# The first block's top layer in two parts of 16 steps, with two products per bank, in a one-core chain of four conditioned layers

## The chip, the cores and the metric

The kernel runs on one core of a Trainium2 chip. The metric is device time in microseconds of one execution. The kernel before took 1318.25 us (median of three runs, 1317.85 to 1321.23).

## What is computed

x is 8 sequences of 512 steps of 256 features; cond is one vector of 256 per sequence. Four residual layers follow each other, all in float32:

```
x = x + L0(x, cond)   # mixture of experts: shared SwiGLU + 2 of 8 routed experts
x = x + L1(x, cond)   # Haar transform, gate(cond), inverse: a gate per feature
x = x + L2(x, cond)   # adapter: low-rank factors generated from cond, gelu between
x = x + L3(x, cond)   # GRU over the 512 steps, output projection
```

L0: `shared = (silu(x sw1') * (x sw3')) sw2`; the router takes `sigmoid(x router' + cond router_t')`, picks two of eight experts per token and weighs `gelu(x rw1[e]') rw2[e]'`. L1 comes down to x times a number per sequence and feature. L2: `mid = gelu(x down + (x a2) b2)`, `x + mid up' + a1 (b1 mid)`, with a1, b1, a2, b2 from a small network on cond whose last matrix w2 has 8 MB. L3, in each step: `Z = s(xz + H Whz')`, `R = s(xr + H Whr')`, `H' = tanh(xh + (R*H) Whh')`, `H = Z*H + (1-Z)*H'`, output `H Whq'`. The step is serial: 512 of them stand one behind the other.

## The kernel before

**Blocks.** The 512 steps are cut into 16 blocks (windows, `w`) of WS = 32 steps; with 8 sequences a block has NT = 256 columns. For each block the top layer L0 and the lower layers L1 and L2 are computed with features on the partitions, as products of 256 columns; the result, turned to steps x sequences, is `xt`, and the recurrence L3 reads it through `project` (L1228), four steps at a time and five steps ahead. Every product is four matmuls on four column tiles of 32 (`quads`, L482). The first two blocks' lower layers are already cut into two halves of 16 steps (HALVED = 2, `lower`, L656).

**Planner.** L0 to L2 are written as jobs with an engine, dependencies, buffers (`Ring`, `Lazy`) and an assumed length (TAKES, L60). `Jobs.run` (L181) plays them against an assumed clock until a given set is done: this lays down the prologue's order on every engine. The prologue ends when the top layer of block 0, the generated factors and the weights are planned (L1156), then the first half of block 0's lower layers (L1314) and AHEAD = 1 further PE job (L1315). From there the recurrence is written out step by step (L1362 on), and in each step `first_slot` (L1334) and `second_slot` (L1342) say how many waiting PE jobs go before and after the candidate's products. `behind` (L1328) compares the jobs left with a straight line that ends at step 462. Engines work in order, so a job that isn't ready when its turn comes holds all that stands behind it.

**Top layer** (`window_jobs`, L497). Four pairs of hidden products with sw1 and sw3, each pair in a PSUM bank `hp` or `low` of two halves (sig on ACT L583, lin and g on DVE L591, L599), then eight experts, two per bank (sig L617, gl L625, and the gate product on GpSimd L634 with `bc`, the gates spread over the partitions). All go into one bank `acc` through sw2 and rw2 (`into_acc`, L537).

**Gates** (`route`, L903). Router products into a bank, some 25 small operations on DVE (in the queue `small`, behind all others), a transpose to `cT`, a store to DRAM (`comb_d`, L990) and four broadcasting loads per block into `bc` (L517).

**Generator** (L1081 to L1142). w2 is loaded in eight pieces of 1 MB, three of them into the space of a later x load, five through a ring of four buffers, so the eighth piece's load waits until a buffer is read (L418). For each of two factor pairs n: bias rows and 2 x 16 products into the bank `misc` (L1104), a copy to low_out, two transposes through `grh`, a copy to low_in. The lower layers of a part need low_in[0] and low_out[0] for down, low_in[1] and low_out[1] for up.

**Loads** go in order on SP's queue: x of block 0 (half k = 0), sw13 (k = 0), x (k = 1), sw13 (k = 1), x of blocks 1 to 3, sw2, rw1, wsq_a, rw2, w2's eight pieces, wx, wh, the rest of x, then broadcasts. Small things go by ACT's and GpSimd's queues.

**Recurrence**, per step: r's products (L1197), sigmoid (L1379), transposes (L1393), R*H (L1410), the candidate's products, tanh, transposes, and a scan as the state update (L1469). z's products and d lie beside it. Two lines that set the order of the prologue's end:

```
        jobs.run(ends[0][0])
        jobs.run(jobs.queues["PE"][:AHEAD])
```

Of the kernel before, what the change touches and what calls it, by code (L numbers as in the profile page):

```python
# [51 lines left out]
HALVED = 2  # L52
# [10 lines left out]
AHEAD = 1  # L63
# [74 lines left out]
class Jobs:  # L138


    def __init__(self):
        self.queues = {e: [] for e in TAKES}
        self.urgent = {e: [] for e in TAKES}
        self.last = {e: [] for e in TAKES}
        self.small = {e: [] for e in TAKES}
        self.clock = {e: 0.0 for e in TAKES}
        self.now = 0.0
        self.ending = lambda: not self.left("PE")
# [32 lines left out]
    def run(self, until):  # L181

        while any(j.done is None for j in until):
            for eng, at in self.clock.items():
                if at <= self.now:
                    qs = (self.queues[eng], self.small[eng])
                    ready = ((j, q) for q in qs for j in q if j.ready(self.now))
                    job, q = next(ready, (None, None))
                    if job is not None:
                        q.remove(job)  # L190
                        job.emit(self.now)
                        self.clock[eng] = self.now + job.takes
            self.now += 0.02
# [10 lines left out]
def cond_resid_kernel(  # L204
# [49 lines left out]
    TAKES["PE"] = PE_ALONE  # L254
# [22 lines left out]
    r_g = ring("g", [P, NT], 6)  # L277
# [36 lines left out]

    jobs = Jobs()
    jobs.clock["PE"] = 3.5
# [36 lines left out]
    def load_x(n, mb, some=None, between=None):  # L353
# [12 lines left out]
        for k in range(KC):  # L366
            got.append(load(t[:, k, :, a:b], xs[:, k, :, t0 + a : t0 + b], mb))
            if between is not None:
                between(k)
# [8 lines left out]
    def load_sw13(k):  # L378
        rows = sw13[:, ts(k, P), :].rearrange("g p h -> p g h")
        got_sw13.append(load(sw13_sb[:, k], rows, 0.5))  # L380


    load_x(0, 0.6, (0, 1), load_sw13)
# [110 lines left out]
    def bt(x):  # L494
        return x.rearrange("p (b t) -> p b t", t=WS)

    def window_jobs(w, routed, xt, via_pool=False):  # L497

        add = jobs.add
        x = xw[w]  # L500

        def mm(lazy, n, lhs, rhs, start, deps, reads=(), tiles=NQ, takes=None):

            return add(
                "PE",
                lambda: quads(lazy.get()[: 32 * tiles, n], lhs(), rhs(), start, tiles),
                deps,
                [lazy, *reads],
                takes,
            )  # L510
# [5 lines left out]
        def fetch(i):  # L516
# [6 lines left out]
            add(  # L523
                "POOL" if via_pool else "SP",
                lambda i=i: fetch(i),
                [routed[w % EARLY], got_w2 if w == 1 else None],
# [6 lines left out]

        acc = Lazy(r_acc)
        order = [None]

        def into_acc(part, lhs, deps, got):  # L537
            for m in range(KC):
                first = order[0] is None
                order[0] = mm(  # L540
                    acc,
                    m,
                    lambda m=m: lhs()[:, ts(m, P)],
                    lambda: part.get(),
                    first,
                    [*deps, got, order[0]],
                    [part],
                )
# [3 lines left out]
        def bank():  # L552

            turn[0] += 1
            return Lazy(r_low if w == 0 and turn[0] % 3 == 0 else r_h)

        def hidden(lazy, n, lhs, got, first=None):

            made = []
            for k in range(KC):  # L560
                made.append(
                    mm(
                        lazy,
                        n,
                        lambda k=k: lhs(k),
                        lambda k=k: x[:, k],
                        k == 0 and first is None,
                        [first, *made, got[k], got_x[w][k]],
                    )
                )  # L570
            return made

        later = []

        for m in range(HC):
            h, sig, lin, g = bank(), Lazy(r_sig), Lazy(r_lin), Lazy(r_g)
            j0, j1 = hidden(h, 0, lambda k, m=m: sw13_sb[:, k, 0, ts(m, P)], got_sw13)
            *_, j3 = hidden(
                h, 1, lambda k, m=m: sw13_sb[:, k, 1, ts(m, P)], got_sw13, j0
            )  # L580
# [7 lines left out]
            )  # L588
            d = add(
# [5 lines left out]
                [h, sig, lin],  # L595
            )
# [4 lines left out]
                [h, lin, g],  # L601
            )
            later.append((g, lambda m=m: sw2_sb[:, m], [d], got_sw2))
# [3 lines left out]
        for e2 in range(0, E, 2):  # L607
            h, j0 = bank(), None
            for n in range(2):
                e = e2 + n  # L610
                got = [got_rw1[e // (E // 2)]] * KC
                j = hidden(h, n, lambda k, e=e: rw1_sb[:, k, e, :], got, j0)
                j0, j = j
# [16 lines left out]
                    queue=None if w else jobs.small,  # L630
                )
                p = add(
                    "POOL",
                    lambda gl=gl, g=g, e=e: nc.gpsimd.tensor_tensor(  # L634
                        g.get(), gl.get(), bcs[e // 2].get()[:, e % 2], ALU.mult
                    ),
                    [d, fetched[e // 2]],
                    [gl, g, bcs[e // 2]],
                )
                later.append((g, lambda e=e: rw2_sb[:, e], [p], got_rw2))  # L640
                if len(later) > 3:
                    into_acc(*later.pop(0))
        for part in later:
            into_acc(*part)
        l0_ends.append(order[0])


        x1, x2, mid = Lazy(r_x1), Lazy(r_x2), Lazy(r_mid)
        turned = []
        halves = 2 if w < HALVED else 1  # L650
        for half in range(halves):
            at = slice(half * WS // halves, (half + 1) * WS // halves)
            turned.append(lower(w, at, acc, x1, x2, mid, xt, order[0]))
        return turned

    def lower(w, at, acc, x1, x2, mid, xt, got_acc):  # L656

        add = jobs.add
        n_t = at.stop - at.start
        x = xw[w][:, :, :, at]  # L660
        whole = n_t == WS
        scale = n_t / WS

        def of(z, m):
            v = z.get()[:, m]
            return v if whole else bt(v)[:, :, at]

        def of3(z, m):
            return bt(z.get()[:, m])[:, :, at]

        def units(products, deps, lazies):

            last, made = None, []
            step = 1 if whole else 2
            for a in range(0, len(products), step):
                group = products[a : a + step]
                last = add(
                    "PE",
                    lambda group=group: [f() for f in group],
                    [*deps, last],  # L680
                    lazies,
                )
                made.extend([last] * len(group))
            return made

        done = []
        for m in range(KC):
            d = add(
                "DVE",
                lambda m=m: stt(of3(x1, m), of3(acc, m), THIRD, x[:, m], ALU.mult, ALU.add),  # L690
                [got_acc],
                [acc, x1],
                TAKES["DVE"] * (0.4 + 0.6 * scale),
# [4 lines left out]
                    lambda m=m: nc.gpsimd.tensor_tensor(  # L698
                        of3(x2, m),
                        of3(x1, m),  # L700
                        lr2[:, m, :].rearrange("p (b o) -> p b o", o=1).broadcast_to([P, B, n_t]),
# [4 lines left out]
                    TAKES["POOL"] * (0.2 + 0.8 * scale),  # L706
                )
            )

        def mul(out, n, lhs, rhs, start, tiles=NQ):  # L710
            o = out.get()[: 32 * tiles, n]
            quads(o if whole else bt(o)[:, :, at], lhs, rhs, start, tiles)

        def adapted(out, n, src, base, deps):
# [4 lines left out]
                    lambda k=k: mul(lu, 0, low_in[:, n, k, :], of(src, k), k == 0, 2)  # L719
                    for k in range(KC)  # L720
# [4 lines left out]
            u = us[n]  # L725

# [3 lines left out]
                    bt(u[:BR])[:, :, at],  # L730
                    bt(lu.get()[:BR, 0])[:, :, at],
# [5 lines left out]
                TAKES["DVE"] * (0.4 + 0.6 * scale),  # L737
# [3 lines left out]
                    lambda k=k, m=m: mul(  # L741
                        out, m, wsq_a[:, k, base, ts(m, P)], of(src, k), m == 0 and k == 0
                    )
                    for m in range(KC)
                    for k in range(KC)
# [4 lines left out]
            return units(  # L750
                [
                    lambda m=m: mul(
                        out, m, low_out[:, n, ts(m, P)], u if whole else bt(u)[:, :, at], False
                    )
# [4 lines left out]
            )  # L759

# [3 lines left out]
        for m in range(KC):  # L764
# [5 lines left out]
                    bt(sig.get())[:, :, at], of3(mid_ps, m), AF.Erf, scale=0.5 * RSQRT2  # L770
# [3 lines left out]
                TAKES["ACT"] * (0.4 + 0.6 * scale),  # L774
# [5 lines left out]
                        of3(mid, m), bt(sig.get())[:, :, at], 1.0, of3(mid_ps, m), ALU.add, ALU.mult  # L780
# [3 lines left out]
                    TAKES["DVE"] * (0.4 + 0.6 * scale),  # L784
# [5 lines left out]
        for m in range(KC):  # L790
            d = add(
                "DVE",
                lambda m=m: stt(x[:, m], of3(up_ps, m), 0.25, of3(x2, m), ALU.mult, ALU.add),
                [ends[m]],
                [up_ps, x2],
                TAKES["DVE"] * (0.4 + 0.6 * scale),
            )

            def turn(m=m, copy=nc.gpsimd.tensor_copy):
                return copy(xt.get()[:, m, at, :], x[:, m].rearrange("p b t -> p t b"))  # L800


            if w == 0 and not whole and at.start == 0 and m:
# [758 lines left out]
```

## Time and profile before

| | us |
|---|---|
| median of three runs | 1318.25 |
| the profiled execution | 1318.28 |
| its span in the profile | 1316.5 |
| busy: PE / weight loads / DVE / ACT / GpSimd | 1178.3 / 688.4 / 916.8 / 505.7 / 150.6 |
| projection for step 0 begins | 65.25 |
| scan of the first step ends | 69.73 |
| scan of the last step ends | 1310.91 |
| logits' transpose, cT's transpose (start) | 18.25, 28.22 |
| bc of block 0 landed, four transfers | 40.77 to 44.88 |
| eighth piece of w2: issue, landing | 43.02, 47.9 |
| wh landed, last of four | 56.71 |

Busy times overlap; a PE that is busy is not a PE at its peak, as matmuls are pipelined. In the profile each float32 product shows as two matmul and two weight-load records, so "x32" stands for 16 of the program's products; in the chain of waits loads and matmuls are counted together. "idle <-" behind a row names what ended the engine's wait. The landings are the times at which a transfer's semaphore reached its count.

### The profile page before, as it was taken

The page shows a single profiled execution, that of the slowest core. Times are in us where ns is not written, and L with a number is a line of the kernel's source. Part 1 is how long each engine was busy: PE and PEld are TensorE (multiplying, and loading weights), DVE is VectorE, ACT ScalarE, POOL GpSimd, SP SyncE. Part 2 cuts the span into 40 slices and gives each one's busy share as a digit, 9 for nine tenths or more (in the row PEclk, how much of TensorE's full clock was granted, in tenths as well). Part 3 has the DMA queues.
Part 4 walks back from the last instruction along what each step waited for, and adds up shares of the span by engine and source line. Part 5 has one row for each costly group of instructions (what it writes and reads, how often), then busy time and mean ns, then how long its engine had stood idle before and what let it go on. Part 6 is the DMA issues. An engine that isn't in the chain of part 4 may idle for free.

```text
span 1316.5 us, 88999 instructions
## 1 busy us (share of the span) xinstructions
PE 1178.3 (89%) x39240; PEld 688.4 (52%) x39240; DVE 916.8 (70%) x6271; ACT 505.7 (38%) x3407; POOL 150.6 (11%) x235
## 2 busy tenths in 40 slices
PE   8999999899999999998888988888888888878886
PEld 5666555555555555555554555545554545545443
DVE  5367777777776767676776767677676767667775
ACT  2134343444344444334343433443434344433332
POOL 3311110101011110101011010101101011110000
PEclk9999999999999999999999999999999999999999
DMA  9910001200010010100000010000001000000111
GB/s 318 352 53 16 5 4 38 52 5 29 13 36 20 12 29 5 52 4 28 12 15 26 4 36 4 22 19 12 28 4 29 12 4 4 4 4 4 36 30 26
DMA packets 41859, 46.46 MB, mean 35 GB/s; under 512 B 27488, under 2 KB 31104, under 8 KB 40320
## 3 DMA queue, kind: packets, MB, share of 16 engines
q1 hardware_dynamic: 38576, 38.31, 9.5%
q8 instruction: 306, 5.01, 1.6%
q0 software_dynamic: 1184, 2.31, 0.5%
q14 instruction: 81, 0.66, 0.2%
q10 hardware_dynamic: 1712, 0.16, 0.1%
HBM read 36.45 MB, written 4.33 MB: 31 GB/s over the span
## 4 chain that ended last, share of the span: by engine, by line
PE 66%; DVE 19%; ACT 9%; issue 4%; DMA 2%; SPq 0%; ACTq 0%
PE grh L1197 35%; PE hp L485 11%; DVE d L1393 7%; DVE rT L1393 6%; PE acc L485 6%; PE gz L1197 5%; ACT c L1379 5%; PE low L485 4%; ACT r L1379 4%; PE misc L485 3%; DVE s_h L1469 3%; DVE s_rh L1410 2%; DMA bc<-comb_d 1%; DMA sw_sb<-in_sw_dram 0%; PE misc L1104 0%
## 5 line engine op out<-in xcount | busy, mean ns | idle before, releaser
L1393 DVE STREAM_TRANSPOSE rT<-r 128x32 f32<-128x32 f32 x1024 | 156.1, 191 | 219.5 <-ACT r L1379 215.8
L1379 ACT ACTIVATE r<-grh 128x32 f32<-128x32 f32 x1024 | 146.3, 195 | 421.0 <-PE grh L1197 418.2
L1197 PE MATMUL grh<-wh,s_h 128*32 128x64 f32 x8192 | 221.8, 225 | 90.1 <-DVE s_h L1469 89.1
L1197 PEld LDWEIGHTS grh<-wh,s_h 128*32 128x32 f32 x8192 | 140.4, 109 | 309.6 <-DVE s_h L1469 308.4
L1379 ACT ACTIVATE c<-grh 128x32 f32<-128x32 f32 x1024 | 146.2, 195 | 313.6 <-PE grh L1197 313.1
L1197 PE MATMUL grh<-wh,s_rh 128*32 128x64 f32 x8192 | 221.6, 225 | 34.3 <-DVE s_rh L1410 10.0
L1197 PEld LDWEIGHTS grh<-wh,s_rh 128*32 128x32 f32 x8192 | 139.2, 108 | 191.8 <-DVE s_rh L1410 188.1
L1393 DVE STREAM_TRANSPOSE d<-c 128x32 f32<-128x32 f32 x1024 | 156.5, 192 | 115.2 <-ACT c L1379 108.9
L1197 PE MATMUL gz<-wh,s_h 128*32 128x64 f32 x8192 | 209.9, 219 | 0.4 <-issue 0.3
L1197 PEld LDWEIGHTS gz<-wh,s_h 128*32 128x32 f32 x8192 | 153.5, 110 | 0.9 <-issue 0.8
L485 PE MATMUL acc<-g,rw_sb 128*32 128x256 f32 x2048 | 153.5, 379 | 0.0
L485 PE MATMUL hp<-x,sw_sb 128*32 128x256 f32 x2016 | 150.8, 384 | 2.6 <-ACT sig L583 2.2
L634 POOL TENSOR_TENSOR g<-gl,bc 128x256 f32<-128x256 f32 x128 | 93.6, 733 | 511.9 <-DVE s_h L1469 358.8
L485 PE MATMUL hp<-x,rw_sb 128*32 128x256 f32 x2016 | 151.4, 380 | 0.7 <-ACT sig L617 0.6
L1469 DVE TENSOR_TENSOR_SCAN s_h<-d,d 128x16 f32<-128x16 f32 x1024 | 145.4, 184 | 0.0
L1410 DVE TENSOR_TENSOR s_rh<-rT,s_h 128x8 f32<-128x8 f32 x1024 | 133.5, 168 | 0.0
L1393 DVE STREAM_TRANSPOSE zT<-z 128x64 f32<-128x64 f32 x512 | 121.9, 238 | 0.4 <-ACT z L1379 0.3
L1379 ACT ACTIVATE z<-gz 128x64 f32<-128x64 f32 x512 | 121.4, 237 | 0.8 <-PE gz L1197 0.4
L1483 ACT COPY hist<-s_h 128x16 f32<-128x16 f32 x512 | 106.3, 208 | 0.5 <-DVE s_h L1469 0.5
L1197 PE MATMUL grh<-wx,xt 128*32 128x128 f32 x2048 | 104.8, 274 | 1.3 <-ACT r L1379 1.1
L1422 DVE TENSOR_TENSOR d<-zT,s_h 128x16 f32<-128x16 f32 x512 | 90.7, 177 | 17.5
L1423 DVE TENSOR_SCALAR d<-zT 128x16 f32<-128x16 f32 x512 | 86.8, 169 | 0.0
(154 smaller groups left out, 1208.7 us busy)
## 6 DMA issues: line engine op xcount, KB each, us to landing
bc<-comb_d SPq DMA_DIRECT2D x56, 256.0 KB, 3.2
w<-in_w_dram SPq DMA_DIRECT2D x5, 1024.0 KB, 13.5
out_dram<-x SPq DMA_DIRECT2D x14, 256.0 KB, 3.2
x<-in_w_dram SPq DMA_DIRECT2D x3, 1024.0 KB, 15.6
x<-in_xT_dram SPq DMA_DIRECT2D x2, 1536.0 KB
bc<-comb_d POOLq DMA_DIRECT2D x8, 256.0 KB, 9.0
sw_sb<-in_sw_dram SPq DMA_DIRECT2D x3, 512.0 KB, 8.0
wsq_a<-in_sq_a_dram SPq DMA_DIRECT2D x1, 1280.0 KB
```

The costliest lines, as they stand in the source:

```text
L485: nc.tensor.matmul(out[ts(j, 32)], lhs[:, ts(j, 32)], rhs, start=start, stop=False, skip_group_check=True,)
L634: lambda gl=gl, g=g, e=e: nc.gpsimd.tensor_tensor(g.get(), gl.get(), bcs[e // 2].get()[:, e % 2], ALU.mult),
L1197: nc.tensor.matmul(out[ts(j, 32)], lhs, rhs[:, ..., ts(j, FQ)], start=start, stop=False, skip_group_check=True,)
L1379: nc.scalar.activation(x, y, func)
L1393: ins = nc.vector.transpose(dst.rearrange("p i u b -> p i (u b)"), src.rearrange("p (i r) -> p i r", r=32),)
L1410: prod = tt(s_rh[u][:, k, u, :], rT[:, k, u, :], h[:, k], ALU.mult)
L1422: tt(d1[:, :, u, :, 1], zT[:, :, u, :], h, ALU.mult)
L1423: nc.vector.tensor_scalar(d0[:, :, :, 1], zT[:, :, u, :], -1.0, 1.0, ALU.mult, ALU.add)
L1469: new = nc.vector.tensor_tensor_scan(s_h[v][:, k, v].rearrange("p b w -> p (b w)"), d0[:, k].rearrange("p b w -> p (b w)"), d1[:, k, u].re ...
L1483: nc.scalar.copy(hist[:, :, t, :], s_h[v][:, :, v, :, 1])
```

## The change

What it does, part by part. (1) Block 0's top layer is computed in two parts of 16 steps as well (L0_PARTS), each followed by its own lower layers; so a product of block 0 has 128 columns. (2) Two such products share the half of a bank that one product had, so that ACT, DVE and GpSimd still work on 256 columns at a time; a class `Part` does the slicing, for the lower layers of blocks 0 and 1 too, whose two feature halves now lie in one operation. (3) The second factor pair's generator uses the bank `grh` (r_c) in place of `misc`, and follows the first pair's low_in. (4) x of block 0 is loaded ahead of sw13, both halves. (5) For block 0 the router's DVE operations go in the main queue, and part 1's lin and g in a new queue `first` ahead of it. (6) The buffers g become 5, with 4 of their own (gs) for the shared expert. (7) While PE has nothing ready before 10 us of the assumed clock it adds zero products to `gz`. (8) The prologue ends when PE has AHEAD = 7 jobs fewer than at the plan's readiness of part 1. (9) In the recurrence the slots take one and two jobs whenever the work is more than FAR = 16 jobs behind. (10) The layer norm's deviation and its use are two jobs.

```
-HALVED = 2
+L0_PARTS = {0: 2}
+LOWER_PARTS = {0: 2, 1: 2}
...
-AHEAD = 1
+WARM = 10.0
+AHEAD = 7
+FAR = 16
...
-    def run(self, until):
+    def run(self, until, left=None):
-        while any(j.done is None for j in until):
+        while any(j.done is None for j in until) or left is not None and self.left("PE") > left:
...
-                    qs = (self.queues[eng], self.small[eng])
+                    qs = (self.first[eng], self.queues[eng], self.small[eng])
...
+                    elif eng == "PE" and self.now < WARM:
+                        self.idle()
+                        self.clock[eng] = self.now + TAKES[eng]
...
-    r_g = ring("g", [P, NT], 6)
+    r_g = ring("g", [P, NT], 5)
+    r_gs = ring("gs", [P, NT], 4)
...
-    load_x(0, 0.6, (0, 1), load_sw13)
+    load_x(0, 0.45, (0, 1))
+    for k in range(KC):
+        load_sw13(k)
...
+        l0 = parts(L0_PARTS.get(w, 1))
+        made = []
+        for part in parts(LOWER_PARTS.get(w, 1)):
+            if len(l0) > len(made):
+                acc, got = l0_jobs(l0[len(made)], bcs, fetched)
...
+            made.append(lower_jobs(part, acc, acc_of, got, xt))
+        return made
+
+    class Part:
...
+        def __init__(self, w, at):
+            self.w, self.at, self.n_t = w, at, at.stop - at.start
+            self.n_c = B * self.n_t
+            self.per = NT // self.n_c
+            self.x = xw[w][:, :, :, at]
+            self.first = w == 0 and not at.start
+
+        def of(self, z, m):
+            return flat(z)[:, m * self.n_c : (m + 1) * self.n_c]
...
+        def units(self, products, deps, lazies):
+
+            last, made = None, []
+            for a in range(0, len(products), self.per):
+                group = products[a : a + self.per]
+                more = [d for _, ds in group for d in ds]
+                last = jobs.add(
+                    "PE",
+                    lambda group=group: [f() for f, _ in group],
+                    [*deps, *more, last],
+                    lazies,
+                )
+                made.extend([last] * len(group))
+            return made
...
-        for m in range(HC):
-            h, sig, lin, g = bank(), Lazy(r_sig), Lazy(r_lin), Lazy(r_g)
+        for m in range(0, HC, per):
+            h, sig, lin, g = bank(), Lazy(r_sig), Lazy(r_lin), Lazy(r_gs)
...
+            queue = jobs.first if first_part else None
...
-        for e2 in range(0, E, 2):
+        for e2 in range(0, E, 2 * per):
...
+                def weigh(gl=gl, g=g, e=e):
+                    gates = bcs[e // 2].get()[:, e % 2 : e % 2 + per]
+                    gates = gates.rearrange("p e (b t) -> p e b t", t=WS)[:, :, :, at]
+                    return nc.gpsimd.tensor_tensor(
+                        all_of(g, 0), all_of(gl, 0), gates, ALU.mult
+                    )
...
-            d = jobs.add("DVE", fn, [d, got_rbias], (), takes, jobs.small)
+            d = jobs.add("DVE", fn, [d, got_rbias], (), takes, jobs.small if first else None)
...
-        gp = Lazy(r_m)
+        gp = Lazy(r_c if n else r_m)
...
-        j = pe(biased_rows, [got_b2, got_sq_a], [gp], 0.45)
+        j = pe(biased_rows, [got_b2, got_sq_a, got_low_in[0]], [gp], 0.45)
...
-        jobs.run(jobs.queues["PE"][:AHEAD])
+        jobs.run([], jobs.left("PE") - AHEAD)
...
             if jobs.left("PE"):
+                if behind(s, FAR):
+                    return 1
                 return 1 if behind(s) and jobs.ready("PE", at + 1.0) > 1 else 0
...
+            if behind(s, FAR):
+                return 2
             two = behind(s, 8) or (s + 5) % 2 == 0 and behind(s)
```

## The prediction, written before the change was run

> **What bounds the kernel now.** I read the page's chain that ended last first. It is one serial path, and its parts are those of a recurrence step.
>
> ```profile
> PE 66%; DVE 19%; ACT 9%; issue 4%; DMA 2%; SPq 0%; ACTq 0%
> ```
>
> Then the same chain in order of time, at its end:
>
> ```profile
> 1305.55 0.30 DVE d L1393 x2
> 1306.04 0.48 PE grh L1197 x16
> 1306.77 0.30 DVE rT L1393 x2
> 1307.23 0.47 PE grh L1197 x16
> 1307.96 0.31 DVE d L1393 x2
> ```
>
> From one candidate transpose to the next are 2.41 us: that is a step, bound by its own latency. By the scans' ends in the trace the first step ends at 69.73 and the last at 1310.91: 1241.18 us for 511 steps. The median step is 2.418, 1235.6 in all; the other 5.6 us are holes, above all at steps 1 (1.33), 4 (0.70), 13 (0.47), 60 (1.17) and 286 (0.35). After the last scan come 5.6 us of output. So the kernel is prologue + 512 steps + tail, and only the prologue and the holes can be shortened. Third, busy time by stage:
>
> ```profile
> 7.50:27.00 19.50, 17.76 (x244) 9.46 (x244) 9.91 (x40) 4.05 (x9) 4.22 (x8) 1.00 1.05 355
> 27.00:46.00 19.00, 18.42 (x304) 11.08 (x307) 7.29 (x29) 3.60 (x11) 6.39 (x11) 1.00 0.97 391
> 46.00:65.25 19.25, 18.14 (x388) 12.35 (x380) 7.07 (x33) 2.62 (x8) 6.15 (x12) 1.00 1.04 334
> 65.25:69.73 4.48, 3.63 (x155) 2.97 (x145) 1.53 (x12) 0.69 (x5) 0.00 (x0) 1.00 0.69 261
> ```
>
> The columns are PE, weight loads, DVE, ACT, POOL, clock, DMA share, GB/s. PE and DMA are both nearly full up to 65.25, where the projection for step 0 begins, and the clock is full. Which of the two ends last is in the chain and in SP's queue:
>
> ```profile
> 41.23 1.73 PE misc L1104 x32
> 42.95 0.43 PE hp L485 x8
> ...
> 46.91 1.73 PE misc L1104 x32
> 48.64 1.24 PE acc L485 x21
> 49.88 17.88 DMA bc<-comb_d
> ```
>
> ```profile
> 30.09 13.25 SPq L323 DMA_DIRECT2D w<-in_w_dram  x2
> 43.39 1.87 SPq L323 DMA_DIRECT2D wx<-in_sq_b_dram  x3
> 45.30 1.92 SPq L323 DMA_DIRECT2D wh<-in_sq_b_dram  x4
> ```
>
> The 17.88 us of "DMA bc" I don't take at its word: PE works all through that stretch in the timeline, and the waits on r's activation are for transfers long landed. SP's row says more: the eighth generator piece is issued at 43.02, when the generator's run of 41.23 to 42.95 frees its buffer; wx and wh stand behind it. By the trace's semaphores piece seven lands at 44.15, eight at 47.9, wh at 56.71. PE reaches the use of piece eight only at 51.70: here PE is the later one, by 3.8 us.
>
> **Products in halves.** In the rows of one product per bank, 16 generator products (x32; the trace shows each twice) take 1.73 us, so a product of 256 columns costs 0.108, a job of four 0.43. Is one of 128 columns half of that? The lower layers of the kernel before have that very form, 8 by 16 strided:
>
> ```profile
> L485 PEld LDWEIGHTS low<-x,wsq_a x32: 106/110/110, 58.7 to 59.6; 128*32 128x32 f32 x32
> L485 PE MATMUL low<-x,wsq_a x32: 272/273/297, 58.7 to 59.7; 128*32 128x128 f32 x32
> ```
>
> The first starts at 58.71, the next group at 59.61: 16 products in 0.87 us, 0.0545 each, each with its own weight load. Recurrence products of 64 columns go at 0.027. The Trainium skill ("TensorE: Matmul & The Clock Gate", Back-to-back issue gap) speaks against the change here: in a stream of load and product pairs it gives about 81 ns at 128 columns and 131 at 512. Linear between these, 256 would cost 98, so half the columns would still cost 83% of the time. The first block's top layer becomes 256 + 192 = 448 half products. By the row they cost 448 x (0.0545 - 0.0538) = 0.3 us more than before, by the page 448 x (0.83 - 0.50) x 0.108 = 16.0 us more. I take the row: same shape, type and four column tiles.
>
> **PE's work ahead of step 0.** From the two programs' orders, with these durations. Before, from the first hp product to the projection: hidden products 20.6 (twelve banks at 1.72, four of block 1), acc 11.6, generator and its bias rows 8.1, conditioning 3.9, router 0.86, transposes 0.74, lower layers 3.7: 49.5 us, in 57.65 (7.60 to 65.25), so 8.2 idle. After: part 1's hidden 6.9, part 2's 6.9, acc 5.2 + 5.2, generator 8.1, conditioning 3.0, router 0.86, transposes 0.74, part 1's lower 3.0, a dummy run 0.4, and nine jobs of block 1 (3.9): 44.0. The difference is deferred, not removed: block 1's products (8.2 to 3.9), part 2's lower work (0.65), and a conditioning run (0.95) that now lies in the wait for sw13.
>
> **Walking the new order.** Times of landings are those before, durations of rows above. sw13's second half lands at 10.8 (both x pieces now go ahead of sw13, same bytes); hp_1 and hp_2 are done at 13.4, the router at 14.3 (before 18.2). DVE's 23 router operations at 0.257 now go in its main queue, behind both banks' products: cT at 21.9 (before 28.7). Its round trip through DRAM took 5.0 us to landing, then 0.3, then 6.5 to 9 for the four broadcasts: gates at 34 to 38 (before 40.8 to 44.9). PE waits for sw2 (14.9) and rw1 (17.2, 19.0) and about 1.2 for the g1 chain, and gets to the generator's second half at 35.8, when its piece (34.99) is there; end 37.5. SP can then issue piece eight at 37.6 instead of 43.0. It cannot land before seven (44.15) plus 1 MB at the 0.42 MB/us seen there: 46.6. acc_1 closes at 43.7, DVE 0.42 and POOL 0.73 make x2 by 45.0. PE stands before the generator's last half at 46.0 and, being in order, holds everything behind it until 46.6: low_2, transposes, the rest of acc_2.
>
> From 46.6 PE has 1.73 + 0.86 + 0.37 + 0.43 + 1.72 + 0.22 + 0.86 + 0.43 + 0.43 + 1.72 + 1.72 = 10.5 us, with 0.3 of wait for mid (DVE makes it behind brow and 12 memsets, 1.6 us in its rows): projection at 57.4. The last 3.9 of these are jobs of block 1 and part 2, queued ahead of a projection whose xt is ready at 54.5 (DVE 0.42 and ACT 0.42 behind low_3's end at 53.5). The walk knows no small stalls; the kernel before had some 0.5 each on ACT's sigmoids. I add 0.8: 58.2, so 7.0 earlier. Step 0 itself keeps its 4.48.
>
> **What hides the rest.** wh: its last transfer took 9.9 to landing (9.1 to 9.9 in the tile's answer). Issue is bounded by piece seven on its lane, 44.2, so 53 to 56; it is needed at 60. If it slips beyond 60, start slips one for one. The second generator bank removes a conflict: the low product of part 1 uses misc while generator 2 fills grh. Without it low_2's chain would stand behind generator 2's copy, some 1.7. POOL's gate products now read strided gates: 0.73 as before, or up to twice; four of them before acc_1 would give 2.9 at most, and gates have 4 us to spare. WARM's zero products run before sw13 is there, in PE's idle time, at nothing; the clock is 1.00 already. The rings of g hold nine buffers in place of six, so no product waits longer for one. GpSimd issues block 1's four broadcasts behind x2, at 45 (before 47.9); they took 9 to land, and their first user stands in step 10. ACT's three stores of cT come before nothing that PE needs within 1 us. The split layer norm is the same nine operations: 0.
>
> **The steps.** Per step at most 0.63 us of other PE work precedes the candidate's products and 0.94 follows, before and after alike, except step 4 (1.26 in both: claim). The 96 heaviest steps of before (1.4 us and more of such work) have the same median, 2.418, as the lightest. Woven work rises from 545 to 550 us, mostly in steps 32 to 63; it fits empty slots, and FAR only fills slots earlier: 0. But steps 0 to 3 now overlap x_rest and the broadcasts, which in the before ran into step 0 only. The hole of 1.20 "issue" at 69.33 lies in that traffic. The skill ("Runtime: NRT & Kernel Launch", Instruction fetch mechanics) calls fetching instructions mostly hidden; that would make it 0. The rows show holes of 1.2, thus 0 to 2.4 more; I take 0.5, nearer none since 60 and 286 have holes without the traffic.
>
> **Sum.** The profiled execution took 1318.28 (span 1316.5, 1.8 around it), the median 1318.25: no difference. -7.0 + 0.5 = -6.5: 1311.7.
>
> **Rivals.**
> 1. As computed, 58%: projection between 57 and 59.5, time 1310 to 1314.
> 2. Given back, 22%: PE reaches the last generator half at 49 to 51, not 46 (idle as before, 8 us), or three more fetch holes. For: before idled 8.2 in 58. Against: the landing at 46.6 absorbs the first of it. Gain 1.5 to 4: 1314.3 to 1317; the lower end could touch no change.
> 3. More, 10%: piece eight lands at 45.5, no stall, step 1's hole goes: 1307.5 to 1310.
> 4. Slower, 6%: half products cost what the page says. 16.0 us in place of 0.3 in the prologue, less 0.6 of slack before piece eight: 1311.7 + 15.1 = 1327. It decides from 6.5/448 = 15 ns extra on each.
> 5. It does little, 4%: wh or the gates are late in the new traffic and step 0 begins at 64 to 66: 1317 to 1320.
>
> A difference under 0.3% (4 us) can hardly be told from none. Faster (below 1314.3): 58 + 10 and a few of rival 2: 0.74. Same: 0.18. Slower: 0.08. Range 1307.5 to 1317.
>
> **What would show it.** First scan's end near 62.7 (69.73); cT by 23; bc landed by 39; piece eight issued before 40; 16 half products in 0.9 us; steps at 2.418; tail 5.6. Wrong if the first scan ends after 66, if half products take over 70 ns, or if steps 0 to 30 add over 3 us.

## The result

The changed kernel takes 1329.21 us (median of six runs, 1326.86 to 1331.14) against 1318.08 for the kernel before (median of six, 1317.85 to 1321.23): 1.0078 times the time before, 95% interval 1.0068 to 1.0089. The prediction was 1311.7, with 1307.5 to 1317 as its range. The kernel became slower, not faster.

The profiled execution has a span of 1327.7. Its first scan ends at 80.14 (before 69.73), its last at 1322.17 (1310.91). The median step is 2.418, the holes of the steps (what their distances add up to over 511 times 2.418) are 6.4 us (5.6), and 5.6 us of output follow. So 10.4 of the 11.2 us of span that were lost lie ahead of the end of step 0. The projection begins at 75.30 (65.25).

### The profile page after: what moved, and what is told of

The parts are those of the page before. It is cut to its first block, busy times and chain, and to the rows that moved or that the text cites. A ratio compares the mean times of both kernels' runs of the same rounds, so it can differ in the third digit from the quotient of the medians.

```text
span 1327.7 us, 89970 instructions
## 1 busy us (share of the span) xinstructions
PE 1187.1 (89%) x39736; PEld 705.5 (53%) x39736; DVE 915.7 (69%) x6259; ACT 506.1 (38%) x3403; POOL 149.4 (11%) x228
## 4 chain that ended last, share of the span: by engine, by line
PE 68%; DVE 18%; ACT 9%; issue 5%; ACTq 0%; DVEq 0%
PE grh L1271 35%; PE hp L507 11%; DVE d L1471 7%; PE acc L507 6%; DVE rT L1471 6%; PE gz L1271 5%; ACT c L1457 5%; PE low L507 5%; ACT r L1457 4%; PE misc L507 3%; DVE s_h L1547 3%; DVE s_rh L1488 2%; ACT sig L704 0%; PE misc L1177 0%; PE grh L1177 0%
## 5 line engine op out<-in xcount | busy, mean ns | idle before, releaser
L507 PE MATMUL hp<-x,sw_sb 128*32 128x256 f32 (+1 forms) x2176 | 156.3, 374 | 2.5 <-ACT sig L666 2.1
L507 PE MATMUL acc<-g,rw_sb 128*32 128x256 f32 (+1 forms) x2176 | 156.6, 370 | 0.9 <-issue 0.9
L507 PE MATMUL hp<-x,rw_sb 128*32 128x256 f32 (+1 forms) x2112 | 154.3, 374 | 1.8 <-ACT sig L704 1.1
```

The lines of the kernel that those rows point to most:

```text
L507: nc.tensor.matmul(out[ts(j, 32)], lhs[:, ts(j, 32)], rhs, start=start, stop=False, skip_group_check=True,)
```

## The profile after

The chain's shares by engine hardly differ (PE 68%, "issue" 5%). Busy time by stage; the columns are as in the prediction (PE, weight loads, DVE, ACT, POOL, clock, DMA share, GB/s):

```profile
7.50:27.00 19.50, 16.16 (x360) 13.52 (x363) 9.48 (x41) 3.67 (x8) 4.24 (x8) 0.92 1.06 373
27.00:46.00 19.00, 15.91 (x352) 13.04 (x348) 6.00 (x24) 2.85 (x9) 5.85 (x9) 0.91 0.82 339
46.00:75.30 29.30, 24.70 (x605) 19.34 (x600) 6.40 (x28) 3.05 (x8) 6.00 (x10) 0.94 0.88 278
75.30:80.14 4.84, 3.88 (x151) 3.09 (x146) 1.85 (x14) 1.07 (x6) 0.00 (x0) 1.00 0.04 14
```

Two things are new. PE is idle for 16 or 17% of each stage ahead of the projection, where it was 3 to 9%, and the granted clock is no longer 1.00. The chain in order of time says what the idle time is:

```profile
19.71 1.35 PE low L507 x48
21.82 1.28 issue
...
41.12 2.18 PE hp L507 x78
43.29 0.61 issue
...
59.57 0.87 PE low L507 x32
61.14 3.11 issue
65.00 3.20 PE acc L507 x60
```

"Issue" is time in which PE waited for nothing that the profile shows: 1.28, 0.61 and 3.11 here, and with smaller ones that end at 29.1, 55.9 and 70.5 in all 6.25 us ahead of the projection. The three stretches of low clock, of 3.41 us each:

```profile
23.70:27.10 3.40, 2.86 (x59) 2.36 (x51) 1.15 (x6) 0.77 (x2) 0.53 (x1) 0.50 1.02 419
33.90:37.30 3.40, 3.40 (x52) 2.77 (x52) 0.96 (x4) 0.22 (x1) 0.00 (x0) 0.51 1.00 417
64.70:68.10 3.40, 3.40 (x72) 3.37 (x66) 0.42 (x1) 0.39 (x1) 0.00 (x0) 0.50 1.07 393
```

Each stands behind an idle stretch: the hole at 21.8 with a wait for ACT, the wait of 1.13 for g1 that ends at 33.28, the hole at 61.1. PE is busy for 9.66 us in them at half the clock, so they cost about 4.8, as an estimate. The kernel before has no such stretch between 13.8 us and its last step.

What does "issue" hide? The trace lists the instruction transfers on a queue of their own:

```profile
q8 instruction: 310, 5.08, 1.6%
```

310 packets of 16 KB, for 39736 matmul records (two to a product) in the page: 64 products to a packet, or block. A half product on its tile takes 0.0545 us, so PE uses up a block in 3.5 us; of the whole products before, at 0.108, a block lasted 6.9.

The packets lie in the trace with their start and length, and I set them against PE's records. Number the blocks from 0. In the kernel before, up to 80 us, block i begins to come when PE has done i + 0.7 to i + 1.0 blocks; only at 63.60 and 68.08 is it later, i + 1.27 and i + 1.44, and its one large hole follows. In the changed kernel it is i + 1.66 at 20.55, i + 1.70 at 61.80 and i + 1.50 at 74.19. The packet of 61.80 lies inside the hole of 61.14 to 64.25. It is no single case: in all traces of this study together PE has 37 "issue" holes of over 0.25 us up to 82 us, and each of them ends 1.2 to 1.8 us behind the end of such a packet. PE stands until a block has come. In the changed kernel's prologue the blocks begin 6.1 to 8.9 us apart, and only once closer, 3.51, at 45.05, where the DMA queues have next to nothing left to move: a first hint that traffic delays them.

## Experiments

Theory A: PE's instructions come too late. Half products use up a block twice as fast, beside full DMA traffic the next block isn't there, PE stands, and (theory B) the clock is halved behind the standstill. Rival C: it is the new order of the work, with its waits. Runs of one table share their runs of before, whose medians were 1319.75, 1320.02 and 1319.54 in the three tables. I compare by the ratios, a tenth of a per cent being 1.3 us; by its ratio the changed kernel loses 10.3 us. A first scan's end is of one profile, and profiles differ in how long PE's clock stays at half speed at the start (up to 13.8 us in the kernel before, 13.5 in the changed one, 4 to 14 in the others), which can move it: by some 3 us in an estimate, half of the 6.2 us from the first hidden product to 13.8 in the kernel before.

### Undo the split; the split alone; move a transfer; fill a wait

Undo the split:

```
-L0_PARTS = {0: 2}
+L0_PARTS = {}
```

> The changed kernel with L0_PARTS empty: block 0's top layer is whole again, products of 256 columns, everything else of the change stays. Theory A (instruction supply: half products use up a 16 KB block of PE's instructions twice as fast, in the full DMA traffic of the prologue the next block lands too late, PE stands still, and its clock is then halved for 3.41 us): no 'issue' hole over 0.7 us ahead of the projection, no halved clock, first scan's end 66 to 71, time 1315 to 1320. Theory C (the new order itself: first queue, loads, generator bank, seven jobs ahead of the projection): first scan's end 76 to 80, time 1325 to 1329.

Half products in the order of before (`cut` takes half the columns):

```
+                if w:
+                    return quads(o, lhs(), rhs(), start, tiles)
+                for i in range(2):
+                    quads(cut(o, i), lhs(), cut(rhs(), i), start and not i, tiles)
```

> The kernel before, in its own order, with every product of block 0's top layer issued as two of 128 columns, 224 matmul instructions more and nothing else. Theory A: 448 half products at 0.060 to 0.062 us, thus 2.7 to 3.7 us more of PE work, and holes and halved clock windows on top: first scan's end 4 to 9 us later than 69.7, time 1322 to 1327. Theory C: 0.3 to 1 us more, time 1318.5 to 1319.5. The page's price for a half product (16 us more): 1334.

The rest of x later:

```
-        nc.vector.tensor_copy(s_h[0][:, :, 0, :, 1], h0)
+        begun = nc.vector.tensor_copy(s_h[0][:, :, 0, :, 1], h0)
+        for j in rest:
+            after(j.emit(base), begun)
```

> The changed kernel with the load of the rest of x (two transfers of 1.5 MB) held until h0 is copied at the projection. Theory A: the hole of 3.11 at 61.1 shrinks under 1 us and the halved clock from 64.7 to 68.1 goes: first scan's end at 75 to 76.5, time 1324 to 1326. Theory C: nothing moves, 1328.5 to 1329.5.

Zero products in g1's wait:

```
+            if w == A_L1W2:
+                claim_half(0)
+                claim_half(1)
```

> The changed kernel with eight zero products of 256 columns (0.86 us of PE) in front of the product that waits 1.13 us for g1. Theory B (the clock follows how busy PE was in the 3.41 us before): the halved clock from 33.9 to 37.4 goes, PE reaches the generator's second half 1.4 us earlier, time 1327.5 to 1328.3. Theory A without B (the halved clock has another origin): the halved stretch stays, time 1329 to 1329.5.

| run | median | ratio to before (95%) | first scan's end, one profile |
|---|---|---|---|
| no split | 1326.04 | 1.0041 (1.0025 to 1.0057) | 74.39 |
| halves in the old order | 1329.12 | 1.0070 (1.0053 to 1.0087) | 80.65 |
| rest of x later | 1330.17 | 1.0075 (1.0058 to 1.0092) | 74.21 |
| zeros in g1's wait | 1328.76 | 1.0062 (1.0042 to 1.0082) | 75.19 |

The second run decides against C as the main cause: 224 matmul instructions more, the order of before, and 9.2 us are lost, more than A expected (1327 at most). PE's waits up to 80 us in it, in sum, times, longest:

```profile
PE low L485 <- issue: 2.6, 2, 1.9
PE acc L485 <- issue: 2.4, 1, 2.4
...
PE grh L1208 <- issue: 1.0, 1, 1.0
PE misc L1115 <- issue: 0.8, 1, 0.8
```

The kernel before has one "issue" hole over 0.3 in that time, of 1.20. The third run is a miss for the total and a hit for the place: the hole at x's rest went from 3.11 to 1.74 (under 1 had been expected), and step 2, where the transfers now lay, became 3.3 us longer. The holes follow the traffic. The fourth is a hit for B's mechanism: with PE kept busy, the stretch behind g1's wait has the full clock,

```profile
34.40:37.80 3.40, 2.84 (x84) 2.12 (x76) 1.27 (x3) 0.77 (x2) 0.73 (x1) 1.00 1.01 420
```

but the gain, 2 us by the ratios, is within their intervals (the profile is of the fastest of its four executions). The first run went against A: without the split, still 5.4 us are lost. Its profile shows one hole and one low stretch behind it, at the rest of x:

```profile
63.40:65.90 2.50, 0.03 (x1) 0.00 (x0) 0.00 (x0) 0.00 (x0) 0.00 (x0) 0.93 1.03 376
65.90:69.00 3.10, 3.06 (x39) 2.12 (x38) 0.42 (x1) 0.39 (x1) 0.00 (x0) 0.50 0.64 241
```

So something else in the change costs too, and the two losses, 5.4 without the split and 9.2 by the halves alone, don't simply add up to the 10.3.

### The same sums with a quarter of the instructions

A product is four matmuls on column tiles of 32. As one matmul over 128 columns it does the same with one instruction for four:

```
+    def one(out, lhs, rhs, start):
+        nc.tensor.matmul(
+            out, lhs, rhs, start=start, stop=False, skip_group_check=True
+        )
...
+        mul = quads if w else one
```

> The changed kernel with every product of block 0's top layer as one matmul over all 128 output columns in place of four on column tiles of 32: 112 matmul instructions in place of 448 for the same sums in the same order. Theory A (instruction supply): PE uses up a block of its instructions far more slowly, no hole over 1 us ahead of the projection, no halved clock after the first 10 us; if the one matmul takes the 0.218 us of the four, first scan's end 69 to 72 and time 1317 to 1321. Theory C (the order of the work): first scan's end 78 to 80, time 1327 to 1330. If a full-width matmul is slower than its four tiles, by twice say, PE has 24 us more ahead of step 0 and the time is over 1340.

> The changed kernel without the split of the top layer and with AHEAD = 1 as before. Against the run without the split alone (1326.0): if the six further jobs ahead of the projection are what it lost, first scan's end 70 to 71.5 and time 1321 to 1323. If it lost to the other parts (loads, first queue, generator bank), 1325 to 1327.

> The kernel before with every four-tile product of all blocks as one matmul over 128 output columns, a quarter of the instructions in the same order. Theory A: the holes of the prologue's end and of the steps go (5.6 us in the steps), first scan's end 68 to 69.5, time 1312 to 1316. If instruction supply is no limit there: 1318 to 1320. If a full-width matmul is slower than four tiles: over 1340.

> The changed kernel with every four-tile product of all blocks, generator and lower layers too, as one matmul over 128 output columns. Theory A: no hole and no halved clock ahead of the projection, first scan's end 65 to 70, holes of the steps under 3 us, time 1309 to 1317. Theory C: 1326 to 1330. If a full-width matmul is slower than four tiles: over 1340.

The second has AHEAD = 1 beside the empty L0_PARTS; the last two put the same matmul into `quads`.

| run | median | ratio to before (95%) | first scan's end |
|---|---|---|---|
| one matmul per product, block 0's top layer | 1322.02 | 1.0015 (1.0003 to 1.0027) | 70.22 |
| no split, AHEAD = 1 | 1322.70 | 1.0016 (1.0009 to 1.0024) | 72.87 |
| one matmul everywhere, before | 1422.39 | 1.0767 (1.0751 to 1.0783) | 69.53 |
| one matmul everywhere, after | 1423.21 | 1.0789 (1.0761 to 1.0817) | 68.80 |

The first is the decisive one: the changed kernel's order, its products and its sums, a quarter of the instructions for them, and 8.3 of the 10.3 us are back (the median is 1 us over the range that A had named). The waits of PE up to 80 us have no "issue" ahead of the projection:

```profile
PE hp L517 <- ACT sig L672: 1.5, 3, 0.5
PE grh L1113 <- DVE g L1149: 1.1, 1, 1.1
PE hp L517 <- ACT sig L710: 1.1, 2, 0.5
PE gz L1277 <- issue: 0.8, 1, 0.8
```

(the 0.8 is at 71.5, in step 1). One stretch of low clock is left, 6.83 us from 29.66, behind the wait for g1. In a stream the one matmul costs about what the four cost: eight of them lie between 15.11 and 16.99 in the trace of the run with zeros, below, 0.235 each against 4 x 0.0545 = 0.218. Woven into the steps it is worse by far: the median step is 2.646 in place of 2.418 in the third run, and the two runs that have it everywhere lose over 100 us, so they tell nothing of the supply. The second run says that 3.3 of the 5.4 us which the kernel without the split had lost, give or take 2 by the intervals, are the six further jobs ahead of the projection. Its profile is of an execution 4 us over its median, so its first scan's end of 72.87 is not typical.

### What is left

Zeros in g1's wait beside the one matmul; then x's rest in six pieces; that alone in the kernel before; and in the kernel without the split:

```
+                if rest and s % 3 == 2:
+                    after(rest.pop(0).emit(at), new)
```

> The run with one matmul per product of block 0's top layer (1322.0), and twelve zero products of 256 columns (1.29 us of PE) in front of the product that waits 1.12 us for g1. Theory B: the two halved windows from 29.7 to 36.5, 6.8 us with 3 us lost, go; PE reaches the generator's second half by 40 in place of 42.3; time 1319 to 1320. If the halved clock costs nothing at the end, because something else comes late: 1321.5 to 1322.5.

> As the run with one matmul per product and zeros in g1's wait, and the rest of x loaded in six pieces of 0.5 MB, one every third step from step 2 on, in place of two of 1.5 MB ahead of step 0. Theory A: the holes of the steps 0 to 30 (4.0 us in the run with one matmul per product) fall under 1.5 us, and none comes ahead of step 0; 2 to 3 us less: 1316 to 1318. If the holes have nothing to do with these transfers: 1319 to 1320.

> The kernel before, and nothing but the rest of x loaded in six pieces, one every third step from step 2 on. Theory A: its holes at the projection and at the steps 1, 4 and 13 (1.2 and 2.5 us) go for the most part: 1315.5 to 1318. If traffic isn't their cause: within 0.5 us of the kernel before.

> The changed kernel without the split of the top layer and with AHEAD = 1 (1322.7), and the rest of x in six pieces, one every third step. Theory A: the hole of 2.45 at the projection and those of the steps 1 to 6 (2.6 us) go: 1318 to 1320. If what it lost lies in the loads ahead or in the router's place, 1322 to 1323.

| run | median | ratio to before (95%) | first scan's end | holes of the steps |
|---|---|---|---|---|
| one matmul, zeros | 1320.60 | 1.0010 (1.0000 to 1.0019) | 67.16 | 8.2 |
| one matmul, zeros, x in pieces | 1320.61 | 1.0003 (0.9992 to 1.0013) | 69.47 | 8.0 |
| before, x in pieces | 1318.65 | 0.9993 (0.9984 to 1.0001) | 68.50 | 5.8 |
| no split, AHEAD = 1, x in pieces | 1322.49 | 1.0017 (1.0009 to 1.0025) | 70.71 | 8.4 |

The holes of this table are against steps of 2.418. With both costs taken away the changed order equals the kernel before, and no more. B is seen again (no low stretch after 4.2 us in the first profile); its gain, 0.7 us by the ratios, is within the intervals, so how much of the time the halved clock costs is not shown by the medians. Spreading x removed the holes of the first steps (1.7 us) in the second run, and others came later in that execution: a miss, the medians don't move. In the kernel before it gives 0.9 us that can't be told from none.

### Supply measured by itself, and three leftovers

640 zero products of 16 columns stand at the end of the kernel before, in the quiet and beside 8 MB of copies:

```
+        for i in range(640):
+            nc.tensor.matmul(
+                gz.rearrange("p c n f -> p (c n f)")[ts(i % NQ, 32), :16],
+                zeros[:, 0:32],
+                zeros[:, :16],
...
```

> The kernel before, followed by 640 zero products of 16 columns behind the last output products, when hardly a transfer runs: 10 blocks of instructions. If PE's supply is bound to about one block in 3.3 us, the shortest distance seen between two blocks in any trace so far: 33 to 36 us for the 640. If supply keeps up in the quiet: about 0.026 us each, 17 us.

> As the run of 640 tiny products, and beside them 8 MB of copies from DRAM to DRAM on two queues from the last scan on. If traffic delays the blocks: 5 to 7 us from block to block while the copies run, 50 to 65 us for the 640. If not: as in the quiet, 33 to 36 us.

The timeline of the first (x128 is 64 products; the brackets hold the idle time ahead of the row),

```profile
1322.17 1.91 PE L1498 MATMUL gz<-zeros 128*32 128x16 f32 x128 [2.12 <-issue]
1325.92 1.91 PE L1498 MATMUL gz<-zeros 128*32 128x16 f32 x128 [1.84 <-issue]
...
1333.71 1.91 PE L1498 MATMUL gz<-zeros 128*32 128x16 f32 x128 [2.13 <-issue]
```

and of the second, while the copies run and just behind them:

```profile
1320.83 1.91 PE L1506 MATMUL gz<-zeros 128*32 128x16 f32 x128 [6.89 <-issue]
1330.88 1.90 PE L1506 MATMUL gz<-zeros 128*32 128x16 f32 x128 [8.14 <-issue]
1339.84 1.90 PE L1506 MATMUL gz<-zeros 128*32 128x16 f32 x128 [7.05 <-issue]
1343.58 1.90 PE L1506 MATMUL gz<-zeros 128*32 128x16 f32 x128 [1.84 <-issue]
```

PE does 64 products in 1.91 us, with its clock at 0.50, then stands until the next 64 are there. The 640 take 34.7 us in the quiet and 52.2 beside the copies, one execution each. A block comes every 3.5 to 4.0 us with hardly a transfer about (3.79 in the mean), and every 9 to 10 us beside the copies (two distances, 10.05 and 8.96); 5 to 7 had been expected. Half products ask for a block in 3.5 us: just more than even the quiet gives. Whole products ask for one in 6.9.

> The kernel before in its own order, with block 0's top layer in products of 128 columns as in the run of half products in the old order (1329.1), but each as one matmul over 128 output columns. Theory A: the whole 9.4 us go, 1319 to 1321, no hole over 1 us ahead of the projection but the one at x's rest. If the halving of the products itself costs, with four times fewer instructions too: over 1324.

> The kernel before, and nothing but the rule FAR = 16 in both slots (one and two jobs whenever the work is more than 16 jobs behind). If the fuller slots use up instruction blocks faster than they come: holes of the steps up from 5.6 to 7 to 9 us, time 1320.5 to 1322. If FAR is free, as predicted: 1319 to 1320, holes 5 to 6.

> The kernel before, with the rest of x in six pieces as in the run that did that alone (1318.65), and the change's zero products ahead of 10 us of the planner's clock. If the clock comes up before 8 us in most executions (13.8 in the kernel before's trace) and PE is what ends last in the prologue: first scan's end 66 to 67.5, time 1316 to 1317.5. If the loads, not PE, end last over the first 20 us: 1318.5 to 1319.5.

```
+                    nc.tensor.matmul(
+                        cut(o, i), lhs(), cut(rhs(), i),
...
+            if behind(s, FAR):
+                return 2
...
+                    elif eng == "PE" and self.now < WARM:
+                        self.idle()
```

Half products as one matmul in the old order: 1322.93, 1.0025 (1.0018 to 1.0032). 5.9 of the 9.2 us are back, not all, and the expectation missed by 2 us. Some of what stays is the one matmul's own price, 112 x (0.235 - 0.218) = 1.9, an estimate; the other 1.4 is open. FAR alone in the kernel before: 1319.01, 0.9995 (0.9987 to 1.0003), free in time, as predicted, with holes of 6.5 us in the steps where 5 to 6 had been expected. Spread x and early zeros in the kernel before: 1320.64, 1.0007 (0.9998 to 1.0016), over both ranges that had been named. The clock came up at 6.0, the first scan ends at 68.72, no earlier than without the zeros (68.50), and PE waits 0.39 for x at 15.0 and 0.82 for sw2 at 16.9: there the loads end last. No version beat the kernel before by more than its interval.

## Why the prediction was wrong

**The bound** held: steps of 2.418, a tail of 5.6, and nearly all of the loss lies in the prologue.

**The price of a half product** held as a price. In the changed kernel 16 of them lie between these starts, 0.87 us, 0.0544 each:

```profile
50.98 1.06 PE L507 MATMUL acc<-g,rw_sb 128*32 128x128 f32 x32
51.85 1.91 PE L1177 MATMUL grh<-w,hid 128*32 128x256 f32 x32
```

The 81 ns for a load and product pair that the Trainium skill gives ("TensorE: Matmul & The Clock Gate", Back-to-back issue gap) is not what this form costs; the row was the better choice.

**The step that failed** is what was made of it: "By the row they cost ... 0.3 us more than before". That sum counts PE's time and leaves out that each of the 448 is an instruction group of its own. The row came from a short group of 16, a quarter of a block. The one place where supply was costed, "I take 0.5, nearer none" with 0 to 2.4 for bounds, looked for holes in the steps 0 to 3 alone, and not in the 50 us ahead, where DMA was full and the rate of instructions doubled. (Rival 2 has "three more fetch holes", also with no sum behind it.) The term measured 6.25 us of holes in the profile, and with the clock behind them 9.2 (halves alone) or 8.3 (given back by one matmul per product). The page the prediction cited ("Runtime: NRT & Kernel Launch", Instruction fetch mechanics) has what was needed, blocks of 16 KiB that are fetched while the one before is executed, and calls the cost of crossing one "mostly hidden"; in these runs that holds only as long as a block lasts longer than its successor takes. The prediction read the adjective and didn't make the division.

The reason for "nearer none" was a misreading too: the hole at step 60 does not lie "without the traffic". In the kernel before four broadcasts of 256 KB run just ahead of it,

```profile
210.50:214.05 3.55, 3.44 (x132) 2.16 (x133) 2.27 (x17) 1.68 (x11) 0.65 (x1) 1.00 0.77 232
```

the next block begins to come at 214.05, late by the count above (i + 1.47), and PE stands from 215.56 to 216.47. So the trace before had the sign: a block that came late beside transfers.

**The clock** was costed "at nothing; the clock is 1.00 already". It was not: between 9.7 and 13.4 the kernel before has 36 matmul records of 256 columns in 3.70 us of busy PE, half the later rate, and the changed one has 73 of 128 columns there, no better, zeros or not. The prediction's own lines disagree here: its sum leaves 8.2 us of idle time, while PE is busy for 54.3 of the 57.65 us in the profile, thus idle for 3.3. Some 2.5 of the 4.9 between are products at half clock before 13.8, an estimate; the rest is open. And later the clock did not stay full behind idle time. The Trainium skill ("TensorE: Matmul & The Clock Gate", Part 1) gives a free-running window of 3.413 us and a halved rate behind an idle one; the trace agrees with the length (3.41) and the grid (23.70, 33.94 and 64.66 lie 3 and 9 windows apart), but here 1.13 us of idle time within a window were enough, not a whole idle one. The three stretches cost about 4.8 us in the profile, by the estimate above; the two runs that filled g1's wait gained 2 and 0.7 us, both within their intervals.

**The walk** expected PE at the generator's second half at 35.8; it came at 46.57. In the run with one matmul and zeros, without holes and low clock, it came at 39.19: 3.4 us of the 10.8 are the walk's own, above all six waits of 0.5 for ACT, for which 0.8 had been added, and only at the end. The other 7.4 are supply and clock, with up to 1.8 of it for that run's early full clock (half of 9.8 to 13.46, an estimate). What hung on it slipped as the text said it would: piece eight was issued at 48.54 (37.6 expected),

```profile
48.54 0.33 SPq L346 DMA_DIRECT2D w<-in_w_dram  x1
48.91 1.67 SPq L346 DMA_DIRECT2D wx<-in_sq_b_dram  x3
50.62 1.89 SPq L346 DMA_DIRECT2D wh<-in_sq_b_dram  x4
```

landed at 53.24 and was used at 57.84, and DMA had idled for it (0.82 in the second stage). wh landed at 63.84. Nothing waited for either. The gates' transpose cT came at 24.6 (21.9 expected), the gates landed at 38.5 to 43.7 in place of 34 to 38, and PE waited for none of them.

**The gain itself.** With supply and clock mended the first scan ends at 67.16 in the better profile, of an execution 2 us under its median. That is 2.6 earlier than before, of the 7.0 expected, and part of the 2.6 is that run's early full clock; the steps' holes, 8.2 in place of 5.6, give it back. Where the rest lies is only partly shown: the ACT waits above, 1.3 us of zeros, six further jobs ahead of the projection (3.3 us by the run without them, in the kernel without the split). Open: the some 2 us (1.2 to 3.2 by the interval) that the kernel without the split still loses at AHEAD = 1. FAR alone was free in the kernel before, and x in pieces didn't bring it back; the order of loads, the router's new place and the generator's second bank weren't tried alone.

**The rivals.** The fourth named 1327 and is nearest, but by luck: it rests on a price that wasn't there, some 36 ns extra on each half product (16.0 us by 448), where the trace has none. The true rival, supply, stood in the text as a detail of the steps.

## What to carry to other kernels

Before cutting products into smaller ones, divide: instructions of a block by the time that PE takes for them, against the time from block to block in the trace, in the stage where the work is done and with its DMA traffic. "Issue" holes on PE together with packets of the instruction queue inside them are the sign of it, and fewer, wider instructions for the same sums are the test. An idle time of 1 to 2 us on PE can cost a second time, by the halved clock behind it; look at the clock of the next window.

## What the hardware showed that was not expected

PE's instructions come in blocks of 64 tiled float32 products, one every 3.5 to 4.0 us in the quiet and every 9 to 10 us beside 8 MB of copies; over all traces of the study no two of PE's blocks begin less than 3.2 us apart. In a stream a float32 matmul over 128 output columns costs 0.235 us at 128 columns moved, as much as its four column tiles within 8%, with a quarter of the instructions; between the products of the recurrence it cost some 0.2 us more per step. PE's clock falls to half in windows of 3.41 us, behind idle time, but by no threshold that these traces give. Every window with more than 2.0 us of PE idle, in all traces, was followed by a halved one. Between 1.1 and 2.0 us it went either way: the wait for g1 (1.12 us of its window) halved the next in all four traces that have it unfilled, while 1.23 us in the kernel before (from 68.43) and 1.89 in the run of halves in the old order (from 24.81) did not. Around the wait for g1 PE is busy with products of 8 columns, 8 records in 1.0 us; whether these count for less is not shown.
